# A graph layer on one core: edge loads of one chunk, eight under way, and more output rows kept to the end

## The chip, the cores and the metric

The kernel runs on one core of one Trainium2 chip. The metric is device time in microseconds of one execution. A core has five engines with instruction queues of their own: TensorE (PE in the profile; its weight loads are shown apart as PEld), VectorE (DVE), ScalarE (ACT), GpSimd (POOL) and SyncE (SP), which here only issues DMAs. SP and POOL both issue DMAs; these are carried out by the same 16 DMA engines.

## The reference

There are 12,500 nodes with 128 features and 412,500 edges with 48 features, sorted by destination node. What is computed:

```
h   = relu(layernorm(x))                            # 12500 x 128
agg = segment_sum(edge_attr, dst)                   # 12500 x 48, sums of edges by destination
u   = graph_globals[0]                              # one row of 64, for all nodes
hid = relu(concat(h, agg, u) @ W1 + b1)             # 240 -> 256
out = x + hid @ W2 + b2                             # 12500 x 128
```

All data are float32. The edges are 79.2 MB, x and the output 6.4 MB each, dst 1.65 MB.

## The kernel before, in words

**Edges.** A chunk is 896 edges: 128 partitions times T = 7 edges, 1344 B in each partition and 168 KB in all. A step `s` is 8 chunks (two halves of four), and there are NS = 58 steps; the last has a half and a tail. Because the edges are sorted, a chunk touches few nodes. DVE compares relative destinations with 0..31 (`onehot`, line 308) and so makes a 0/1 matrix. `aggregate` (334) multiplies it with the edges on TensorE, which sums the edges of each of the 32 nodes of a chunk's window. `keep_sums` (355) copies the sums with ACT, `place_columns` (372) and `place` (378) move them to their node columns with another 0/1 matrix and product, and `add` (386) adds them into `aggT`, the sums by node column, with DVE.

**Twos.** For each of the 7 edge columns `t` of a half, `aggregate` either issues four products of 32 x 48, one per chunk, or two products of 64 x 96, one per pair of chunks, of which the off-diagonal parts are not used. `LEVELS[s]` (608) says how many of the 14 columns of step `s` use the second form ("twos"): up to 7 are in the second half, the rest in the first. A step with any twos has two more small ACT copies in `keep_sums`.

**Nodes.** The rows are handled in 26 blocks: block 0 of 212 rows, 23 blocks of 512 and two of 256. Each is loaded (`load_x`, 393), normalized (DVE and ACT), turned (TensorE), multiplied with the parts of W1 (`first_h`, `first_a`) and W2 (`second`, 518), added to x + b2 by DVE (`result`, 527) and stored (`store`, 536). `plus_b2` (428) adds b2 on POOL. Blocks 0 to 4 (`FIRST`) are begun ahead of the loop, and parts of them are kept in columns of `aggT` not used yet.

**Order.** The order of all instructions is written out by hand (`tc.manual_schedule()`). A planner (`piece`, 707) puts the pieces of blocks into half-steps `k` (two to a step) and `at(k, ...)` lists them; the loop at line 854 then issues each step.

**Edge loads.** SP issues them. `load(s, i)` (297) loads one pair of chunks, 336 KB, into a tile of 2 x 1344 B per partition; there are 18 such tiles. In step `s` the loop calls `load(s + 3, i)` for i = 0..3 at four places. `few` (290) keeps at most FLIGHT = 5 loads of edges, x and dst under way: each waits for the one that is five before it to land. In the loop, each also waits for the matrix product issued last ahead of it ("in TensorE's pace").

**Stores.** For most blocks POOL issues the store half a step after `second`. The blocks in `HELD` (103), the 16 blocks 6 to 21, write their result into columns of `aggT` that are done with, and their stores come in the last three steps, three in each half-step (`k = 2 * (NS - 3) + i // 3`, line 813). Each of these also waits for the matrix product issued last ahead of it. The last three stores (blocks 23 to 25) follow the last products, one from POOL and two from SP.

Of the kernel before, what the change touches and what calls it, by code (L numbers as in the profile page):

```python
# [22 lines left out]
def kernel(  # L23
# [30 lines left out]
    CS = 2 * CH  # L54
# [7 lines left out]
    NS = NSF + 1  # L62
# [33 lines left out]
    NBL = len(blocks)  # L96
# [3 lines left out]

    FIRST = (1, 2, 3, 0, 4)

    HELD = range(NBL - 4 - 16, NBL - 4)
    ZN = 16
    zw = -(-(N + WG) // ZN)

# [36 lines left out]
    def load_edges(e, c, n):  # L143
        return nc.sync.dma_start(
            e[:, :n], edge_attr[c * CE:(c + n) * CE].rearrange("(c p t) d -> p c (t d)", p=P, t=T))
# [4 lines left out]
    def rows_of(ap, a, m, r):  # L150
        return ap[a:a + m * r].rearrange("(p r) d -> p (r d)", r=r)
# [6 lines left out]
    with fast:  # L158
# [131 lines left out]
        def few(now):  # L290
            if len(flight) == FLIGHT:
                tc.add_manual_dep(now.ins, flight.pop(0).ins.name, LANDED, reason="few loads under way")
            flight.append(now)
            if paced:
                tc.add_manual_dep(now.ins, last[0], LANDED, reason="in TensorE's pace")

        def load(s, i):
            if s >= NS or s == NSF and i > 1:
                if s == NSF and i == 2:
                    edges[s].append(etail)  # L300
                return
            for c in (2 * i,):
                e = ep.tile([P, 2, T * DE], F32, name="e")
                few(load_edges(e, s * CS + c, 2))
                edges.setdefault(s, []).extend([e[:, 0], e[:, 1]])
                both.setdefault(s, []).append(e)

# [26 lines left out]
        def aggregate(s, h, twos):  # L334
            left = s == NSF and h
            if h == 0:
                banks_s[s] = ps_agg.tile([P, 512], F32, name="ps")[:, :4 * DE].rearrange("p (h f) -> p h f", h=2)
            ps, es, oh = banks_s[s], edges[s], onehots[s]
            n = TT if left else T
            for t in range(n):  # L340
                first, end = t == 0 and h == 0, t == n - 1
                if t >= n - twos:
                    for q in range(0, CH, 2):
                        c = CH * h + q
                        product(ps[W * q:W * (q + 2), h], oh[:, c // 2, t], both[s][c // 2][:, :, t * DE:(t + 1) * DE],
                                start=first, stop=end, skip_group_check=True)
                    continue
                for q in range(1 if left else CH):
                    c = CH * h + q
                    o = DE * (q % 2) if twos else 0  # L350
                    product(
                        ps[W * q:W * (q + 1), h, o:o + DE], oh[:, c // 2, t, c % 2], es[c][:, t * DE:(t + 1) * DE],
                        start=first, stop=end, skip_group_check=True)
# [32 lines left out]
        def add(s):  # L386
            _, v = nc.values_load_multi_w_load_instructions(  # L387
                at_i[0:1, s:s + 1], engines=[DVE], min_val=low(s), max_val=high(s),
                skip_runtime_bounds_check_because="clamped to these on the chip")
            to = aggT[:HI + DE, ds(v[0], WG)]  # L390
            nc.vector.tensor_tensor(to, to, banks_p.pop(s)[:HI + DE, :WG], OP.add)  # L391
# [135 lines left out]
        def result(j):  # L527
            a, m, r = blocks[j]
            if j in HELD:
                ot = aggT[:, BEFORE + a:BEFORE + a + r * D].rearrange("p (r d) -> p r d", d=D)  # L530
# [5 lines left out]
        def store(j):  # L536
# [3 lines left out]
            for p0, p1 in by_rows(m):  # L540
                now = queue.dma_start(rows_of(out, a + p0 * r, p1 - p0, r), ov[p0:p1])  # L541
                if j in HELD:
                    tc.add_manual_dep(now.ins, last[0], LANDED, reason="edges first")
# [58 lines left out]

        AHEAD = 4
        EARLY = 2
        FLIGHT = 5


        LEVELS = (0, 0, 0, 0, 7, 0, 0, 9, 14, 3, 14, 14, 0, 14, 3, 3, 2, 0, 5, 14, 0, 14, 2, 3, 0, 4, 14, 0, 14, 2, 4, 0, 3, 0, 5, 14, 0, 14, 0, 4, 0, 2, 0, 3, 14, 0, 14, 4, 2, 2, 0, 2, 2, 4, 0, 0, 0, 0)
        LATE = NS - 7
        NEAR = len(FIRST) + 1  # L610
        with tc.manual_schedule():
# [42 lines left out]
            def load_step(s):  # L654
                for i in range(4):
                    load(s, i)
# [3 lines left out]
            load_x(FIRST[1])  # L660
            load_step(0)
            load(1, 0)
            load(1, 1)
            load_x(FIRST[2])
            load(1, 2)
# [28 lines left out]
            def at(k, f, *a):  # L694
                todo.setdefault(max(0, k), []).append((f, a))
# [48 lines left out]
            for i in range(1, len(FIRST)):  # L744
                k = 2 * i
# [38 lines left out]
            for j in range(NW):  # L784
# [8 lines left out]
                if j + 1 < NW:  # L793
                    hidden_x(j + 1)
                    at(where["o", j] + 1, result, j)
                    if j not in HELD:
                        at(where["o", j] + 1, store, j)
# [3 lines left out]
            for j in range(NBL):  # L801
                if j in FIRST:
                    continue
                k = where["turn", j]
# [5 lines left out]
                at(k - 2, normal, j)  # L810
            at(where["a", 0] - 2, bias_of_globals)
            for i, j in enumerate(HELD):
                k = 2 * (NS - 3) + i // 3
                assert where["o", j] + 1 < k
                at(k, store, j)

# [3 lines left out]
            def apart(k, f, *a):  # L820
                while k - 1 in taken or k in taken or k + 1 in taken:
                    k -= 1
                taken.add(k)
                at(k, f, *a)
                return k
# [3 lines left out]
            for i in range(2, len(parts)):  # L829
                need = 2 * (parts[i][0] // CS - (4 if i == len(parts) - 1 else 0))  # L830
                k = apart(need - 4, middles, i)
                at(k + 2, check_dst, i)
                k = apart(k - 1, spread_dst, i, 1)
                k = apart(k - 1, spread_dst, i, 0)
# [5 lines left out]
            k = apart(2 * (NS - 6), verdict)  # L840
# [13 lines left out]
            for s in range(NS):  # L854
# [27 lines left out]
                if s >= LATE:  # L882
                    for p in now:
                        place(p)
                        add(p)
                twos = [max(0, LEVELS[s] - T), min(T, LEVELS[s])]
                aggregate(s, 0, twos[0])
# [37 lines left out]
    with tc.If(isbad >= 1):  # L925
# [3 lines left out]
        with tc.tile_pool(name="any", bufs=1) as ap, tc.tile_pool(  # L929
# [63 lines left out]
            with tc.For_i(0, NCH, 1) as c:  # L993
                e = ap.tile([P, T * DE], F32, name="e2")
                nc.sync.dma_start(e, edge_attr[ds(c * CE, CE)].rearrange("(p t) d -> p (t d)", t=T))
                windows(e, rel[:, ds(c, 1), :].rearrange("p c t -> p (c t)"), ds(c, 1), P)
            e = ap.tile([P, T * DE], F32, name="e3")
# [65 lines left out]
```

## Time and profile before

| | us |
|---|---|
| median of the timed runs | 301.53 |
| timed runs | 299.49, 301.53, 303.27 |
| profiled execution, its own time | 298.43 |
| its span, first to last instruction | 296.6 |
| TensorE busy in it | 283.1 |
| VectorE, ScalarE, GpSimd busy | 237.0, 161.0, 73.7 |
| mean granted clock of TensorE | 0.991 of full speed |

A row of a table by stage holds, for a stretch of the span, the busy time of each engine with its number of instructions, then the clock that TensorE was granted, the mean busy share of the 16 DMA engines (it can pass 1, since packets of one engine overlap) and the GB/s that they moved. A row of waits says which engine and line waited for what: us in total, times, and the longest. A row of a source line gives an instruction's duration as minimum, median and maximum in ns. A row of the chain of waits gives the start, the duration in us, and what ran. A row of DMA issues gives the number of DMAs, KB of each, and the median us from issue to landing.

### The profile page before, as it was taken

How to read it: one execution, taken by the hardware profiler on the slowest of the kernel's cores; microseconds unless marked ns; L12 is line 12 of the kernel's file. 1: busy time of each engine (PE TensorE's matmuls, PEld its weight loads, DVE VectorE, ACT ScalarE, POOL GpSimd, SP SyncE). 2: the span in 40 equal slices, each digit the busy share in tenths (PEclk: the TensorE clock that was granted, in tenths of full speed). 3: DMA queues.
4: the chain of work that ended last, by engine and by line, in shares of the span. 5: the costliest groups of instructions: out<-in, count | busy, mean ns of one | idle time of the engine just before them, and what ended most of it. 6: DMA issues, size and time to landing. Idle time of an engine off the chain costs nothing.

```text
span 296.6 us, 15062 instructions
## 1 busy us (share of the span) xinstructions
PE 283.1 (95%) x6553; PEld 223.5 (75%) x6554; DVE 237.0 (80%) x537; ACT 161.0 (54%) x399; POOL 73.7 (25%) x88
## 2 busy tenths in 40 slices
PE   6799897999999999999999999999999999999992
PEld 2657666898878778878878788867877977787781
DVE  6838969699998997887978699698986799986222
ACT  3477557323756664743666458644651985664420
POOL 3032381130212563021022212021111022103720
PEclk9999998999999999999999999999999999999998
DMA  6999999999999999999999999999999999999962
GB/s 162 372 314 345 272 358 313 370 370 370 356 357 356 326 367 285 298 348 290 332 312 339 346 345 317 336 321 322 310 347 337 353 298 323 337 352 317 363 222 81
DMA packets 69815, 95.19 MB, mean 321 GB/s; under 512 B 5018, under 2 KB 64739, under 8 KB 69743
## 3 DMA queue, kind: packets, MB, share of 16 engines
q1 hardware_dynamic: 67583, 87.66, 89.1%
q0 software_dynamic: 2160, 6.50, 6.1%
q8 instruction: 53, 0.87, 1.2%
q14 instruction: 19, 0.16, 0.1%
HBM read 87.74 MB, written 6.40 MB: 317 GB/s over the span
## 4 chain that ended last, share of the span: by engine, by line
PE 81%; DVE 8%; ACT 3%; DMA 2%; issue 2%; SPq 1%; DVEq 1%
PE ps L195 30%; PE ph L195 21%; PE po L195 14%; PE pp L195 10%; PE pt L199 5%; DVE oh L312 3%; DMA e<-in_edge_attr_dram 2%; DVE place L374 2%; ACT xn L438 1%; ACT hT L452 1%; PE pt L195 1%; DVE st L408 1%; DVE aggT L391 1%; DVE ph L489 1%; DVEq L387 1%
## 5 line engine op out<-in xcount | busy, mean ns | idle before, releaser
L312 DVE TENSOR_TENSOR oh<-iota,rel 128x1792 f32<-128x1792 f32 (+1 forms) x60 | 120.5, 2009 | 0.4 <-ACT rel L270 0.4
L195 PEld LDWEIGHTS ps<-e,oh 128*32 128x32 f32 (+1 forms) x5448 | 94.7, 116 | 21.7 <-issue 5.8
L195 PE MATMUL ps<-e,oh 128*32 128x48 f32 (+1 forms) x5448 | 106.5, 217 | 3.1 <-issue 1.2
L360 ACT COPY sums<-ps 128x192 f32<-128x192 f32 (+2 forms) x129 | 36.7, 285 | 78.7 <-PE ps L195 76.8
L431 POOL TENSOR_TENSOR xb<-xt,b_sb 128x512 f32<-128x512 f32 (+1 forms) x21 | 34.2, 1630 | 131.7 <-DVE aggT L533 79.4
L195 PE MATMUL ph<-hT,w1h 128*128 128x512 f32 (+2 forms) x100 | 49.6, 602 | 0.1
L195 PE MATMUL po<-w,hid 128*128 128x128 f32 (+1 forms) x376 | 48.0, 281 | 0.9 <-ACT hid L516 0.9
L516 ACT ACTIVATE hid<-ph,bias 128x512 f32<-128x512 f32 (+2 forms) x49 | 30.4, 670 | 30.4 <-PE ph L195 22.9
L195 PEld LDWEIGHTS po<-w,hid 128*128 128x128 f32 (+1 forms) x376 | 45.1, 196 | 2.0 <-ACT hid L516 1.3
L391 DVE TENSOR_TENSOR aggT<-aggT,pp 112x246 f32 x58 | 23.6, 406 | 24.5 <-PE pp L195 18.2
L195 PE MATMUL pp<-place,sums 128*112 128x128 f32 x232 | 39.0, 291 | 0.2 <-DVE place L374 0.2
L195 PEld LDWEIGHTS pp<-place,sums 128*112 128x112 f32 x232 | 28.9, 176 | 7.1 <-issue 1.7
L438 ACT ACTIVATE xn<-xt,sh,sc 128x128 f32<-128x128 f32 x80 | 33.1, 483 | 0.3
L374 DVE TENSOR_TENSOR place<-iota,pos 128x256 f32<-128x256 f32 x58 | 32.9, 569 | 0.0
L195 PE MATMUL ph<-aggT,w1a 48*128 48x256 f32 (+1 forms) x192 | 28.6, 402 | 0.2 <-DVE aggT L391 0.2
L195 PEld LDWEIGHTS ph<-aggT,w1a 48*128 48x128 f32 x192 | 17.2, 186 | 10.1 <-issue 6.8
L452 ACT COPY hT<-pt 128x512 f32<-128x512 f32 (+1 forms) x22 | 23.0, 1044 | 3.2 <-PE pt L199 3.1
L195 PEld LDWEIGHTS ph<-hT,w1h 128*128 128x128 f32 x100 | 16.7, 196 | 7.1 <-issue 4.6
L533 DVE TENSOR_TENSOR aggT<-po,xb 128x512 f32<-128x512 f32 x16 | 11.0, 685 | 9.2 <-PE po L195 9.2
L541 POOL DMA_DIRECT2D out_dram<-ot x9 | 5.0, 553 | 51.6 <-DVE ot L533 43.7
L408 DVE BATCH_NORM_STATS2 st<-xt 128x6 f32<-128x128 f32 x80 | 17.3, 277 | 0.0
L199 PE MATMUL pt<-ident,xn 128*128 128x128 f32 x84 | 14.1, 289 | 0.0
(137 smaller groups left out, 188.1 us busy)
## 6 DMA issues: line engine op xcount, KB each, us to landing
e<-in_edge_attr_dram SPq DMA_DIRECT2D x230, 336.0 KB, 5.2
xt<-in_x_dram SPq DMA_DIRECT2D x19, 256.0 KB, 4.9
out_dram<-aggT POOLq DMA_DIRECT2D x16, 256.0 KB, 4.5
out_dram<-ot POOLq DMA_DIRECT2D x7, 256.0 KB, 4.8
di<-in_dst_dram SPq DMA_DIRECT2D x3, 448.0 KB, 5.3
aggT<-in_x_dram SPq DMA_DIRECT2D x4, 256.0 KB, 4.2
xt<-in_x_dram SPq DMA_DIRECT2D x2, 128.0 KB, 4.6
out_dram<-ot SPq DMA_DIRECT2D x2, 128.0 KB, 3.3
```

Of the source, the lines that this page charges most:

```text
L195: last[:] = [nc.tensor.matmul(*a, **k).ins.name]
L199: last[:] = [nc.tensor.transpose(*a, **k).ins.name]
L312: nc.vector.tensor_tensor(to, iota[:, None, :W].to_broadcast([P, n, W]), r[:, :, None].to_broadcast([P, n, W]), OP.is_equal)
L360: nc.scalar.copy(to[k, h], ps[k, h, None, o:o + DE].to_broadcast([k.stop - k.start, h.stop - h.start, 2, DE]))
L374: nc.vector.tensor_tensor(po, iota[:, None, :WP].to_broadcast([P, 2, WP]), pos[:, s, :, None].to_broadcast([P, 2, WP]), OP.is_equal)
L391: nc.vector.tensor_tensor(to, to, banks_p.pop(s)[:HI + DE, :WG], OP.add)
L408: nc.vector.bn_stats(st[:m, q, :], xs[j][:m, q, :])
L431: nc.gpsimd.tensor_tensor(xb[:m, :r], xs[j][:m, :r], b2_sb[:m, None, :].to_broadcast([m, r, D]), OP.add)
L438: nc.scalar.activation(xn[:m, q], xs[j][:m, q], AF.Relu, bias=shift[j][:m, q:q + 1], scale=scale[j][:m, q:q + 1])
L452: nc.scalar.copy(hT[:, :m * r].rearrange("d (p r) -> d r p", r=r), ht[j][:, :m * r].rearrange("d (r p) -> d r p", r=r))
L516: nc.scalar.activation(to, ph, AF.Relu, bias=bias[:, h:h + 1])
L533: nc.vector.tensor_tensor(ot[:m, :r], pos_o[j][:m, :r], xbs[j][:m, :r], OP.add)
```

## The change

Edge loads are issued one chunk at a time, 168 KB, into the two halves of the same tiles, and eight loads may be under way. The stores of blocks 1 to 5 join those held for the last three steps, 21 blocks, now four in each half-step. The list of twos is another one: its sum goes from 248 to 254, and the number of steps that have any from 35 to 33. The number of tiles, the planner, and the places at which loads are issued stay.

```diff
-    HELD = range(NBL - 4 - 16, NBL - 4)
+    HELD = range(1, NBL - 4)
...
             for c in (2 * i,):
                 e = ep.tile([P, 2, T * DE], F32, name="e")
-                few(load_edges(e, s * CS + c, 2))
+                for q in range(2):
+                    few(load_edges(e[:, q:q + 1], s * CS + c + q, 1))
                 edges.setdefault(s, []).extend([e[:, 0], e[:, 1]])
                 both.setdefault(s, []).append(e)
...
-        FLIGHT = 5
-
-
-        LEVELS = (0, 0, 0, 0, 7, 0, 0, 9, 14, 3, 14, 14, 0, 14, 3, 3, 2, 0, 5, 14, 0, 14, 2, 3, 0, 4, 14, 0, 14, 2, 4, 0, 3, 0, 5, 14, 0, 14, 0, 4, 0, 2, 0, 3, 14, 0, 14, 4, 2, 2, 0, 2, 2, 4, 0, 0, 0, 0)
+        FLIGHT = 8
+
+
+        LEVELS = (0, 0, 0, 0, 7, 5, 5, 14, 0, 14, 14, 3, 14, 5, 0, 4, 0, 0, 4, 0, 14, 0, 14, 4, 0, 4, 3, 14, 0, 14, 4, 0, 4, 0, 7, 14, 0, 14, 0, 4, 0, 3, 0, 14, 0, 14, 5, 3, 2, 4, 0, 0, 2, 4, 0, 0, 0, 0)
...
             for i, j in enumerate(HELD):
-                k = 2 * (NS - 3) + i // 3
+                k = 2 * (NS - 3) + i // 4
                 assert where["o", j] + 1 < k
                 at(k, store, j)
```

## The prediction

> **What bounds the kernel now.** I read the page first, then a table by stage, then the waits of TensorE, and last the queue of SP and the chain of waits. The page:
>
> ```profile
> span 296.6 us, 15062 instructions
> ...
> PE 283.1 (95%) x6553; PEld 223.5 (75%) x6554; DVE 237.0 (80%) x537; ACT 161.0 (54%) x399; POOL 73.7 (25%) x88
> ...
> DMA packets 69815, 95.19 MB, mean 321 GB/s; under 512 B 5018, under 2 KB 64739, under 8 KB 69743
> ...
> q1 hardware_dynamic: 67583, 87.66, 89.1%
> q0 software_dynamic: 2160, 6.50, 6.1%
> ...
> PE 81%; DVE 8%; ACT 3%; DMA 2%; issue 2%; SPq 1%; DVEq 1%
> ```
>
> Two resources look full: TensorE is busy 95% of the span, and the two DMA queues together keep the 16 engines busy for 95.2% of it. The table by stage tells which of them sets the pace. Its columns after the stretch are the busy us of PE, PEld, DVE, ACT and POOL, then the granted clock, the DMA share and GB/s:
>
> ```profile
> 31.60:35.00 3.40, 2.50 (x59) 1.87 (x62) 3.33 (x8) 2.28 (x5) 0.92 (x2) 1.00 0.88 230
> 45.70:49.10 3.40, 1.81 (x52) 1.44 (x40) 3.40 (x7) 1.83 (x4) 0.33 (x1) 1.00 0.96 314
> 49.10:52.50 3.40, 3.40 (x50) 3.17 (x53) 3.40 (x4) 2.47 (x8) 0.74 (x2) 0.51 0.93 291
> 49.00:105.00 56.00, 55.84 (x1257) 47.57 (x1257) 51.88 (x107) 30.33 (x79) 15.38 (x18) 0.97 1.04 354
> 105.00:160.00 55.00, 55.00 (x1258) 43.94 (x1254) 45.34 (x95) 31.31 (x76) 11.91 (x10) 1.00 0.98 320
> 160.00:215.00 55.00, 55.00 (x1401) 43.45 (x1400) 47.05 (x100) 30.27 (x74) 11.09 (x9) 1.00 1.00 328
> 215.00:270.00 55.00, 55.00 (x1377) 43.76 (x1376) 46.89 (x113) 33.80 (x91) 9.06 (x8) 1.00 1.00 335
> 274.00:288.00 14.00, 14.00 (x263) 11.17 (x250) 3.50 (x8) 4.90 (x12) 7.22 (x14) 1.00 0.87 318
> 288.00:291.00 3.00, 2.78 (x24) 2.59 (x24) 2.02 (x5) 0.47 (x1) 0.54 (x1) 1.00 0.01 3
> ```
>
> From 105 to 270 us TensorE is busy 165.00 of 165 us, and so are the DMA engines. The waits of TensorE from 12 us on hold one row that names the edges:
>
> ```profile
> PEld ps L195 <- DMA e<-in_edge_attr_dram: 0.5, 2, 0.3
> ```
>
> So in this execution every chunk of edges lands before TensorE wants it. TensorE's own stream sets the end, with the loads just ahead of it. What makes both full at once is the list of twos: a two computes two chunks in one product of 64x96 instead of two of 32x48, and that is the slower form. The chain of waits shows one step without twos (112 matrix instructions) and one with 14 (56):
>
> ```profile
> 230.61 2.46 PE ps L195 x56
> ...
> 278.54 1.33 PE ps L195 x112
> ```
>
> Fourteen twos cost 2.46 - 1.33 = 1.13 us, 0.081 us each. The list of before has 248 of them (summed from the code), about 20 us of filling that uses up TensorE's time while edges arrive.
>
> **The change part by part.**
>
> *The list of twos.* The sum rises from 248 to 254. Steps 5 and 6 get 5 each. Steps 7 to 9 go from 9, 14, 3 to 14, 0, 14, two more. From step 10 on the sum falls from 215 to 209. The last is on the path: 6 x 0.081 = -0.49 us. The two more of steps 7 to 9 cost +0.16 us. The ten of steps 5 and 6 fall where TensorE idles: from 45.7 to 49.1 us it is busy 1.81 of 3.40 us, idle for 1.59, while DVE is busy all 3.40. Ten twos are 0.81 us, so I cost them at nothing; with that cover gone they would cost +0.81. Behind this idle stretch the granted clock falls to 0.51 from 49.1 to 52.5 us, which loses 3.40 x 0.49 = 1.67 us of full-speed work on a TensorE that is busy throughout. With 0.81 us more work the idle time before it comes to 0.78 us. The stretch from 31.6 to 35.0 us, idle for 0.90 us, was followed by no fall (its own clock is 1.00 and the next fall is at 49). I take the fall as gone: -1.67 us, between -1.67 and 0 (0 if it comes all the same, a little later). The Trainium skill, "TensorE: Matmul & The Clock Gate", section "What's actually happening", says that the clock gate judges activity by free-running windows of some 3.4 us; by that the fall could turn on where the window lies, and the term would be 0 in some executions. The trace agrees with the length (0.51 over 3.4 us). Two steps fewer have twos at all, so ACT makes four small copies fewer, off the path at 54% busy.
>
> *One chunk a load, eight under way.* SP issues 460 edge loads in place of 230. Its queue, by the source view of the load's line and of the x loads' line (ns, min/median/max), and by the chain of waits:
>
> ```profile
> L144 SPq DMA_DIRECT2D e<-in_edge_attr_dram x230: 367/368/1955, 2.6 to 270.8; - x115
> L144 SPq EVENT_SEMAPHORE  x175: 17/17/28, 6.9 to 270.8; - x175
> ...
> DMA to landing us min/median/max: 4.1/5.2/6.8
> ```
>
> ```profile
> L398 SPq DMA_DIRECT2D xt<-in_x_dram x21: 340/341/1072, 43.8 to 246.0; - x21
> ```
>
> ```profile
> 3.12 0.47 SPq L144
> 3.59 0.04 issue
> ```
>
> A load of one chunk has the 128 runs of an x load, so its issue lies near 0.341 us, with a wait of 0.017 and two gaps of 0.04: 0.44 us. At worst it is the 0.47 of the first burst, with the same around it: 0.57. The time there is: 2.6 to 270.8 us, 268.2 us, less some 25 other loads at 0.44 (11 us), leaves 257 us, 0.559 us per chunk. At 0.44 SP needs 202 us and stays ahead; I take that, and no cost. What queues behind a stalled issue on SP is the next edge or x load, and behind those TensorE. The stream has to stay 0.12 us per chunk worse than my value before TensorE waits.
>
> The bytes under way fall from 5 x 336 KB to 8 x 168 KB, by 20%. With five under way a landing of 5.2 us means 5 x 344,064 B / 5.2 us = 331 GB/s, just what the stages show (320 to 335). Eight of half the size give 1.376 MB; for 328 GB/s they must land in 4.2 us. The landings:
>
> ```profile
> e<-in_edge_attr_dram SPq DMA_DIRECT2D x230, 336.0 KB, 5.2
> xt<-in_x_dram SPq DMA_DIRECT2D x19, 256.0 KB, 4.9
> out_dram<-aggT POOLq DMA_DIRECT2D x16, 256.0 KB, 4.5
> ...
> xt<-in_x_dram SPq DMA_DIRECT2D x2, 128.0 KB, 4.6
> out_dram<-ot SPq DMA_DIRECT2D x2, 128.0 KB, 3.3
> ```
>
> Most of a landing is queue: 128 KB of x behind four edge loads take 4.6 us, 128 KB of output at the quiet end 3.3. The queue ahead shrinks by the 20%, and 5.2 x 0.8 = 4.2 us. I take that value, at which the rate holds; the bounds are 3.3 us (417 GB/s, more than the engines move) and 4.7 us (between the two x loads, as if nothing in the queue shrank; 293 GB/s).
>
> Each load also ends in completions. From the two queue rows, 6.1% of 296.6 us x 16 over 2160 packets is 134 ns for 3009 B, and 89.1% over 67583 is 62.6 ns for 1297 B. The line through both is 0.042 ns a byte and 8.5 ns a packet. One small packet more per engine and load is 230 x 8.5 ns = 2.0 us of the engines' time (upper bound 230 x 62.6 ns = 14.4 us, lower 0). The packets under 512 B, 5018, fit 16 to a DMA. The rule that speaks against the change is in the Trainium skill, "DMA: Bandwidth & Descriptors", section "Rules for kernel authors": at least 1 MiB a DMA for bandwidth. Taken with that page's fit in "Anatomy of one DMA" (2.0 us fixed plus bytes over 436 GB/s), an estimate of 2.4 us a chunk with eight under way gives 575 GB/s, so overlapped loads would not be held by it; the sum stays as the rows give it.
>
> *Five more blocks' rows at the end.* Blocks 1 to 5 (256 KB each, 1.31 MB) no longer go out between 49 and 105 us. At that stage's 354 GB/s this is 3.7 us of DMA, so the edges come 3.7 - 2.0 = 1.7 us earlier there. TensorE does not wait for edges in this trace, so on the path it is worth nothing here, at most -1.7 us where it does wait. On POOL five issues leave; nothing behind them there (xb, zeroing) was late for TensorE. At the end:
>
> ```profile
> 272.16 3.21 POOL L541 DMA_DIRECT2D out_dram<-aggT  x6 [3.48 <-PE pt L199]
> ...
> 281.26 2.13 POOL L541 DMA_DIRECT2D out_dram<-aggT  x4 [1.09 <-PE ph L195]
> ```
>
> POOL issues one store in 3.21 / 6 = 0.54 us, 490 GB/s, faster than the engines drain. From 274 to 291 us the engines are idle for 0.13 x 14 + 0.99 x 3 = 4.8 us, and the 3.7 us fit in, ahead of the last three stores at 290.4. I cost this at nothing; if the stores ran over, the last output would be late by up to 3.7 us.
>
> **The sum.** -0.49 + 0.16 - 1.67 = -2.0 us on TensorE's stream. The profiled execution took 298.43 us (span 296.6), so it would take 296.4. The three timed runs of before are 299.49, 301.53 and 303.27; the mean of all four executions is 300.7, and I predict 300.7 - 2.0 = 298.7 us, 1% below the median of 301.53.
>
> **The rivals.**
>
> 1. *The fall of the clock stays, or comes elsewhere.* For it: the ten twos are only 0.81 us, 0.12 us under the one idle stretch that is known to be harmless. Against it: the idle time is halved. Then -0.3 us: 300.4.
>
> 2. *The loads gate the timed runs.* All three lie above the profiled execution, which could be TensorE waiting for edges there. Then relief on the DMA counts as well: -2.0 - 1.7 = -3.7 us, and if completions are free -5.7: 295 to 297. Against it: this trace has 0.5 us of such waits.
>
> 3. *The smaller window starves the DMA engines* (the other side). If a chunk lands in 4.7 us, the rate is 293 in place of 328 GB/s, and the 165 us from 105 to 270 become 165 x 328 / 293 = 185: +20 us, less 1.7 of relief and 2.0 of TensorE, +16: 317 us. It decides from a landing of 4.2 us on, and costs 2% (6 us) from 4.4. For it: x loads half as big land only 0.6 us sooner. Against it: 3.3 us at the quiet end.
>
> 4. *SP becomes the bound.* From 0.559 us a chunk on; at 0.57, 460 x 0.011 = +5 us less 2.0: 304. For it: issues up to 1.955 us in the row. Against it: the median of 0.368 for twice the runs.
>
> 5. *The stores run over the end*: +3.7 - 2.0: 302.
>
> **How the numbers follow.** Forecast 0.47 (296.5 to 301), rival 1 0.18, rival 2 0.15, rival 3 0.08, rival 4 0.07, rival 5 0.05. The range 294.5 to 305 takes in the forecast and rivals 1, 2, 5 and most of 4; left out are rival 3 and the edges of 2 and 4, 0.15. Two per cent of 301.53, about what a measurement of this kernel can tell from no change, is 6 us: faster means under 295.5, slower over 307.6. Faster: half of rival 2 and the low edge of the forecast and of 1, 0.16. Slower: rival 3 and the worse end of 4, 0.12. Within: 0.72.
>
> **What would show it.** Right: no clock under 1.00 between 45 and 56 us; TensorE busy all of 105 to 270; edge landings of about 4.2 us at 320 to 335 GB/s; issues near 0.34 us; packets under 512 B up by some 3,700; the last held store landed before the last three. Wrong: TensorE waits on edges in the hundreds of ns per step (rivals 3, 4: landings of 4.7 us with the DMA share below 0.95, or SP with no waits left), or a DMA share under 0.9 in the middle with TensorE full, which would mean that the filling is now too much and could be cut.

## The result, and the profile after

The changed kernel takes 326.51 us (median of four runs, 322.97 to 330.92) against 301.23 us for the kernel before on the same chip (299.49 to 303.27). The ratio is 1.0731, with a 95% interval from 1.0646 to 1.0817: 7% slower, where 298.7 us was forecast. Two runs of the changed kernel, its profiled execution of 330.92 us among them, were disturbed and are left out of the ratio; the others lie at 322.97 to 323.54 us, so the rows below tell where the time is, and the last 2% of them is not explained.

The page of the changed kernel, with the rows that answer to those of before:

```profile
span 329.2 us, 15276 instructions
...
PE 299.7 (91%) x6529; PEld 233.7 (71%) x6530; DVE 227.3 (69%) x537; ACT 159.3 (48%) x395; POOL 88.6 (27%) x88
...
DMA packets 73497, 95.22 MB, mean 289 GB/s; under 512 B 8698, under 2 KB 68419, under 8 KB 73423
...
q1 hardware_dynamic: 71263, 87.68, 84.9%
...
DMA 46%; PE 37%; SPq 8%; ACT 3%; issue 2%; DVE 2%; DVEq 0%; ACTq 0%
...
e<-in_edge_attr_dram SPq DMA_DIRECT2D x460, 168.0 KB, 4.4
out_dram<-aggT POOLq DMA_DIRECT2D x21, 256.0 KB, 6.3
```

The chain that ends last has changed hands. It was 81% TensorE and 2% DMA; now it is 46% DMA and 37% TensorE. The bytes are the same, but the mean rate has gone from 321 to 289 GB/s, and a load of half the size lands in 4.4 us where the whole one took 5.2. A stretch of the chain of waits shows what that looks like (start, duration, what ran):

```profile
109.61 4.39 DMA e<-in_edge_attr_dram
114.00 0.14 issue
114.14 1.34 PE ps L195 x26
...
118.16 0.43 SPq L144
118.59 0.04 issue
118.63 0.43 SPq L144
...
119.59 4.87 DMA e<-in_edge_attr_dram
124.47 0.04 issue
124.51 1.37 PE ps L195 x26
```

TensorE's products of a step come behind a load that took 4.39, then 4.87 us from its issue to its landing, and in the second case behind issues on SP, one after the other. TensorE itself stands for a part of that time. In its waits from 12 us on, the row that named the edges with 0.5 us before is now this:

```profile
PEld ps L195 <- DMA e<-in_edge_attr_dram: 20.6, 34, 2.4
```

Over the whole span, by the source view of the load's line:

```profile
  PEld ps L195: 21.8, 38
...
  PE ps L195: 16.2, 27
...
DMA to landing us min/median/max: 2.9/4.4/8.9
```

The weight loads of TensorE wait 21.8 us for edges and its products 16.2; these waits overlap in time and can't be added. SP's own waits for landings have nearly gone; the row of before comes first, then that of the changed kernel:

```profile
SPq L144 <- DMA e<-in_edge_attr_dram: 108.2, 176, 2.4
```

```profile
SPq L144 <- DMA e<-in_edge_attr_dram: 11.0, 23, 1.1
```

So SP has little time to spare, and the eight places are not always full. The table by stage says how the loss is spread (busy us of PE, PEld, DVE, ACT and POOL, then granted clock, DMA share, GB/s):

```profile
33.90:37.30 3.40, 3.40 (x61) 3.04 (x50) 2.27 (x3) 0.38 (x2) 1.10 (x1) 0.51 1.05 349
49.10:52.50 3.40, 3.40 (x67) 3.28 (x65) 3.40 (x4) 2.63 (x8) 1.04 (x2) 1.00 1.01 323
49.00:105.00 56.00, 52.42 (x1250) 43.50 (x1249) 46.23 (x95) 26.05 (x65) 16.09 (x12) 1.00 0.99 315
105.00:160.00 55.00, 52.84 (x1125) 41.30 (x1127) 41.18 (x93) 28.34 (x71) 15.37 (x9) 1.00 0.97 301
215.00:270.00 55.00, 52.05 (x1250) 40.42 (x1251) 42.01 (x104) 29.41 (x80) 11.58 (x7) 1.00 0.96 303
300.00:329.20 29.20, 17.72 (x182) 14.02 (x182) 3.57 (x8) 3.17 (x8) 6.49 (x12) 0.68 0.48 185
```

From 49 to 105 us the rate is 315 GB/s, where it was 354, and from there to 270 us some 300, where it was 328. In before, 56 x 354 + 165 x 328 GB/s make 73.9 MB from 49 to 270 us. The changed kernel has moved 56 x 315 = 17.6 MB of that by 105 us and needs 56.3 MB / 300 GB/s = 187.6 us for the rest: it is there at 292.6 us, 22.6 us later. Two things are left out, and they cancel: it came to 49 us with 1.3 MB less (280 GB/s against 306), and 1.3 MB of stores are put off to the end. The difference of its other runs to before is of the same size (323.5 - 301.2 = 22.3), but the rates are those of the profiled execution, which is 32.6 us longer than that of before, so that the close match is in part luck.

TensorE still shows as 91% busy. Its busy time has risen from 283.1 to 299.7 us with 24 matrix instructions fewer. Part of that is the lower clock of this execution (0.966 against 0.991), and the rest looks like waiting that is counted as busy. The number of matrix instructions is the better reading of progress: 3,544 from 105 to 270 us, where before had 4,032.

### The profile page after: what moved, and what is told of

The parts are those of the page before. It is cut to its first block, busy times and chain, and to the rows that moved or that the text cites. A ratio compares the mean times of both kernels' runs of the same rounds, so it can differ in the third digit from the quotient of the medians.

```text
span 329.2 us, 15276 instructions
## 1 busy us (share of the span) xinstructions
PE 299.7 (91%) x6529; PEld 233.7 (71%) x6530; DVE 227.3 (69%) x537; ACT 159.3 (48%) x395; POOL 88.6 (27%) x88
## 2 busy tenths in 40 slices
DMA packets 73497, 95.22 MB, mean 289 GB/s; under 512 B 8698, under 2 KB 68419, under 8 KB 73423
## 4 chain that ended last, share of the span: by engine, by line
DMA 46%; PE 37%; SPq 8%; ACT 3%; issue 2%; DVE 2%; DVEq 0%; ACTq 0%
DMA e<-in_edge_attr_dram 43%; PE ps L195 15%; PE ph L195 9%; SPq L144 8%; PE po L195 6%; PE pp L195 5%; PE pt L199 2%; DMA xt<-in_x_dram 2%; DMA aggT<-in_x_dram 1%; ACT xn L439 1%; ACT hT L453 1%; DVE st L409 1%; PE pt L195 1%; DVE aggT L392 0%; SPq L399 0%
## 5 line engine op out<-in xcount | busy, mean ns | idle before, releaser
L195 PE MATMUL ps<-e,oh 128*32 128x48 f32 (+1 forms) x5424 | 120.6, 219 | 17.6 <-DMA e<-in_edge_attr_dram 16.2
L195 PEld LDWEIGHTS ps<-e,oh 128*32 128x32 f32 (+1 forms) x5424 | 102.8, 117 | 42.1 <-DMA e<-in_edge_attr_dram 21.8
L313 DVE TENSOR_TENSOR oh<-iota,rel 128x1792 f32<-128x1792 f32 (+1 forms) x60 | 117.3, 1956 | 0.4 <-ACT rel L270 0.4
L432 POOL TENSOR_TENSOR xb<-xt,b_sb 128x512 f32<-128x512 f32 (+1 forms) x21 | 49.2, 2341 | 176.0 <-DMA xt<-in_x_dram 126.2
L361 ACT COPY sums<-ps 128x192 f32<-128x192 f32 (+2 forms) x125 | 35.8, 287 | 111.7 <-PE ps L195 110.2
L195 PE MATMUL ph<-hT,w1h 128*128 128x512 f32 (+2 forms) x100 | 50.6, 613 | 0.1
L195 PE MATMUL po<-w,hid 128*128 128x128 f32 (+1 forms) x376 | 47.5, 280 | 0.8 <-ACT hid L517 0.8
L195 PE MATMUL pp<-place,sums 128*112 128x128 f32 x232 | 40.0, 296 | 0.2 <-DVE place L375 0.2
L195 PEld LDWEIGHTS pp<-place,sums 128*112 128x112 f32 x232 | 29.8, 181 | 7.3 <-issue 2.0
L375 DVE TENSOR_TENSOR place<-iota,pos 128x256 f32<-128x256 f32 x58 | 25.4, 440 | 0.0
L542 POOL DMA_DIRECT2D out_dram<-aggT x21 | 11.3, 544 | 9.9 <-DMA out_dram<-aggT 5.8
```

Source lines behind the costliest of these rows:

```text
L195: last[:] = [nc.tensor.matmul(*a, **k).ins.name]
L313: nc.vector.tensor_tensor(to, iota[:, None, :W].to_broadcast([P, n, W]), r[:, :, None].to_broadcast([P, n, W]), OP.is_equal)
L361: nc.scalar.copy(to[k, h], ps[k, h, None, o:o + DE].to_broadcast([k.stop - k.start, h.stop - h.start, 2, DE]))
L375: nc.vector.tensor_tensor(po, iota[:, None, :WP].to_broadcast([P, 2, WP]), pos[:, s, :, None].to_broadcast([P, 2, WP]), OP.is_equal)
L432: nc.gpsimd.tensor_tensor(xb[:m, :r], xs[j][:m, :r], b2_sb[:m, None, :].to_broadcast([m, r, D]), OP.add)
```

## The experiments

Theory A: the bytes under way (1.376 MB instead of 1.72) hold the rate down, since a landing does not shrink in proportion. Theory B: SP's time for twice the issues does. Theory C: the small packets and completions of twice the loads do. Theory D: the list of twos or the held stores do. Edits are made to the kernel before. From most runs the row of the stretch from 105 to 270 us is shown; that of before is

```profile
105.00:270.00 165.00, 165.00 (x4032) 131.15 (x4028) 139.27 (x308) 95.39 (x239) 32.05 (x26) 1.00 0.99 328
```

**The loads alone, and all but the loads.** The first run has only the loads of the change:

```diff
-                few(load_edges(e, s * CS + c, 2))
+                for q in range(2):
+                    few(load_edges(e[:, q:q + 1], s * CS + c + q, 1))
...
-        FLIGHT = 5
+        FLIGHT = 8
```

> The kernel before with only the loads changed (one chunk each, eight under way); the old list of twos and the old 16 held blocks. All three theories of the slow loads (SP's issue; the engines' own cost per load; fewer bytes under way) expect most of the loss here: 316 to 324 us, with edge landings near 4.4 us and about 300 GB/s in the middle. If the stores or the list made the loss, 300 to 303.

Measured: 325.98 us against 301.03, ratio 1.084 (1.0715 to 1.0966).

```profile
105.00:270.00 165.00, 157.38 (x3544) 123.98 (x3543) 123.38 (x282) 87.66 (x219) 39.95 (x28) 0.98 0.95 299
```

That is the whole loss, a little more than the 316 to 324 us expected. The other has the new list of twos (its lines are cut here) and the 21 held blocks, with the loads of before:

```diff
-    HELD = range(NBL - 4 - 16, NBL - 4)
+    HELD = range(1, NBL - 4)
...
-        LEVELS = (0, 0, 0, 0, 7, 0, 0, 9, 14, 3, 14, 14,
+        LEVELS = (0, 0, 0, 0, 7, 5, 5, 14, 0, 14, 14, 3,
...
-                k = 2 * (NS - 3) + i // 3
+                k = 2 * (NS - 3) + i // 4
```

> The changed kernel with the loads put back to pairs of chunks, five under way; the new list and the 21 held blocks stay. By the terms of the prediction for these two (fall of the clock gone -1.67, list -0.33, stores hidden) 298 to 300 us, about 2 below before. If the stores collide with the last edges by themselves, 303 or more.

Measured: 301.67 us against 301.03, ratio 1.0063 (1.0012 to 1.0114).

```profile
34.60:38.00 3.40, 3.40 (x57) 2.94 (x45) 2.15 (x3) 0.47 (x2) 0.00 (x0) 0.50 1.06 349
```

The whole loss is in the loads: theory D falls. The list and the held rows do not bring the 2 us expected either, and the fall of the clock is still there, earlier in the execution (0.50 from 34.6 to 38.0 us, where before has 1.00).

**The same bytes under way with the DMAs of before.** Pairs as before, but four of them:

```diff
-        FLIGHT = 5
+        FLIGHT = 4
```

> The kernel before with four pairs under way in place of five: 1.376 MB, the same bytes under way as eight single chunks, with half as many DMAs. The window theory expects the loss here too: about 300 GB/s, 315 us or more. The issue theory and the engine theory expect no change: landings fall to some 4.2 us, the rate stays 320 to 335 GB/s, 300 to 304 us.

Measured: 329.88 us against 301.03, ratio 1.1024 (1.0914 to 1.1134). The stretch, and then from the page:

```profile
105.00:270.00 165.00, 156.35 (x3549) 123.66 (x3550) 123.24 (x278) 88.45 (x222) 46.33 (x28) 0.98 0.95 300
```

```profile
q1 hardware_dynamic: 67583, 87.66, 84.5%
...
e<-in_edge_attr_dram SPq DMA_DIRECT2D x230, 336.0 KB, 4.6
```

This is the run that decides. It has the issues of before on SP (230) and the packets of before (67,583), so neither B nor C has anything to work with: the smaller window alone is enough for the loss. It may have as many bytes under way as the changed kernel, 4 x 344,064 = 1.376 MB, and it has its rate (300 GB/s), its count of matrix instructions (3,549), and its loss. Four pairs in 4.6 us are 299 GB/s.

**The window put back.** Every other pair is loaded as two singles, with six and with eight loads under way. A load has 229 KB on average, so these are 1.376 and 1.835 MB:

```diff
-                few(load_edges(e, s * CS + c, 2))
+                if i % 2:
+                    for q in range(2):
+                        few(load_edges(e[:, q:q + 1], s * CS + c + q, 1))
+                else:
+                    few(load_edges(e, s * CS + c, 2))
...
-        FLIGHT = 5
+        FLIGHT = 6
```

> The kernel before, in which of the four pair loads of a step two stay pairs and two are split into single chunks; six loads under way, 1.376 MB on the mean, with 345 edge loads. SP has 1.5 issues per pair, well under its limit. The window theory expects the same loss as with four pairs or eight singles: landings such that about 300 GB/s flow, 320 to 330 us. The issue theory expects 300 to 304, the engine theory (a cost per load) about half of the loss, 312.

Measured with six: 318.4 us against 300.88, ratio 1.0576 (1.0507 to 1.0644).

```profile
105.00:270.00 165.00, 155.82 (x3651) 122.99 (x3639) 123.96 (x283) 89.04 (x224) 49.74 (x29) 1.00 0.95 301
```

The same with FLIGHT = 8:

> The same mixed loads with eight under way, 1.83 MB on the mean, somewhat more than the 1.72 MB of before. The window theory expects the rate of before or a little more and 300 to 304 us, although half of the chunks are loaded singly. The engine theory expects half of the loss, about 312, whatever the window.

Measured: 303.91 us against 300.88, ratio 1.0187 (1.0079 to 1.0294).

```profile
105.00:270.00 165.00, 161.85 (x3819) 126.79 (x3818) 133.29 (x301) 91.70 (x231) 29.93 (x25) 1.00 0.98 319
```

These two differ in the window alone and have the same 345 issues. The window is worth 14.5 us between them, and 301 against 319 GB/s. The 1.9% that remains to before may be issues and completions (115 loads more than before, where the changed kernel has 230 more), or what a window wider than 1.72 MB costs by itself, of which more below.

**SP's time.** Is SP harmless, then? Eight empty instructions were put on SP behind each load of a pair:

```diff
                 few(load_edges(e, s * CS + c, 2))
+                for _ in range(8):
+                    nc.sync.drain()
```

> The kernel before with eight empty instructions (drains, some 0.055 us each by the end of the trace of before) on SP behind each pair load: SP's time for a pair goes from about 0.48 to 0.92 us, near that of two single loads (2 x 0.48), with no DMA added. The issue theory expects the loss of the single loads: 312 us or more, SP hardly waiting for landings. The engine and window theories expect 300 to 303 us, with SP's waits for landings cut by about 100 us in total.

Measured: 310.31 us against 301.03, ratio 1.0337 (1.0236 to 1.0437).

```profile
105.00:270.00 165.00, 161.82 (x3818) 128.32 (x3817) 134.45 (x303) 91.84 (x233) 35.55 (x27) 0.99 0.98 317
```

So time on SP does cost, though only a third of the loss and less than the 312 us that theory B asked for. SP waited 12.6 us for landings here, against 108.2 in before: it comes late to a free place, and the window is not full. The other way round, SP was relieved. In the kernel of the first run, every second chunk was issued from ACT's queue:

```diff
-        return nc.sync.dma_start(
+        return (nc.scalar if n == 1 and c % 2 else nc.sync).dma_start(
```

> Single chunks, eight under way, as in the run with the loads alone, but every second one is issued by ACT, so that SP issues 230 edge loads as before the change. The issue theory expects SP's relief to bring back most of the 25 us: 300 to 306. The window theory expects little, since the bytes under way are still at most 1.376 MB: at best the mean under way rises from 7.2 to 8 loads, 315 to 326 us; ACT, which was busy for 161 us, may lose some on top.

Measured: 356.11 us against 302.04, ratio 1.1835 (1.1652 to 1.2018). From the waits:

```profile
PEld ps L195 <- DVE oh L313: 17.3, 2, 15.8
```

The edit did something else as well. TensorE stands for 15.8 us at the start behind a DVE result, with ACT's queue now holding loads that wait for landings in front of ACT's own work (argued from the order on the queue). The run says nothing on SP's share. It was repeated with every fourth chunk from POOL, which has more room:

```diff
-        return nc.sync.dma_start(
+        return (nc.gpsimd if n == 1 and c % 4 == 3 else nc.sync).dma_start(
```

> Single chunks, eight under way, as in the run with the loads alone, but every fourth one is issued by POOL: SP has 345 edge loads. POOL, busy for 74 us, has room for 115 issues of some 0.54 us, though a store or an xb ahead of one in its queue may hold it up. The issue theory expects most of the loss back: 300 to 306. The window theory expects 316 to 326: at most 1.376 MB under way.

Measured: 329.76 us (322.67 to 331.55) against 300.56; its runs lie too far apart for a ratio. The stretch and SP's wait for landings:

```profile
105.00:270.00 165.00, 154.85 (x3552) 121.86 (x3550) 124.00 (x274) 85.28 (x215) 66.73 (x88) 0.99 0.94 299
```

```profile
SPq L144 <- DMA e<-in_edge_attr_dram: 84.0, 105, 4.4
```

SP now has 84.0 us in which it waits for landings (13.1 in the first run), and the rate is 299 GB/s as it was. The places were no fuller for it: by the times of issue and landing in the traces, 7.3 loads were under way on the mean from 105 to 270 us, and 7.2 in the first run. With ten under way (1.72 MB, as in before) in place of eight:

> The same with ten under way, 1.72 MB, the bytes of five pairs. The window theory expects the loss to go: 300 to 306. The engine theory (a cost per load) expects no change against eight: 316 or more. If POOL's queue holds its share up, both of these runs are slow, and then they tell nothing.

Measured: 315.31 us against 300.56, ratio 1.0506 (1.0425 to 1.0588).

```profile
30.00:49.00 19.00, 17.35 (x403) 12.73 (x392) 12.54 (x18) 9.76 (x24) 11.40 (x17) 0.95 0.83 253
...
105.00:270.00 165.00, 159.71 (x3798) 126.12 (x3795) 131.95 (x300) 92.89 (x231) 74.13 (x98) 1.00 0.98 324
```

With the window of before the rate of before is nearly back in this stretch, 324 GB/s, though all loads are single chunks. The time is not: 300 to 306 us were expected. The 5% that stays is spread: the rate is 253 GB/s from 30 to 49 us (318 in before), and TensorE is idle for 5.3 us in the long stretch (0 in before). How much of it is POOL's issues and how much completions was not taken apart. More than eight from SP alone was not tried.

The runs with loads of one size can be put side by side by the bytes that were under way on the mean from 105 to 270 us, and the mean landing of an edge load. Both are worked out from the times of issue and landing in the traces; for up to half of the loads the traces do not tell the landing, and the median of the run is put in.

| | MB under way | landing, us | GB/s |
|---|---|---|---|
| every fourth of eight singles from POOL | 1.30 | 4.4 | 299 |
| changed kernel | 1.33 | 4.4 | 300 |
| four pairs | 1.37 | 4.6 | 300 |
| five pairs, empty instructions on SP | 1.51 | 4.7 | 317 |
| every fourth of ten singles from POOL | 1.52 | 4.7 | 324 |
| five pairs (before) | 1.69 | 5.2 | 328 |

The rate goes with the bytes under way, whether the loads are pairs or singles. SP's time belongs to the same account: a late SP leaves places empty (7.4 of eight are used in the changed kernel, 4.5 of five with the empty instructions). How much of the changed kernel's loss would go with a faster SP was not separated.

**More under way than five pairs.** If the window holds the rate down, does before want a wider one? FLIGHT = 8, FLIGHT = 6, and FLIGHT = 6 with the new list and the held rows:

```diff
-        FLIGHT = 5
+        FLIGHT = 8
```

> The kernel before with eight pairs under way in place of five. From the two landings 4.6 us at 1.37 MB (four pairs) and 5.2 us at 1.70 MB (five), the window theory makes 2.2 us plus 1.77 us per MB, so 7.0 us at 2.75 MB and 390 GB/s, above what the engines have moved in any stage (about 370): the engines become the limit of the loads. TensorE's own stream with its twos is then alone in setting the end: 297 to 300 us. If the engines were already full at five, landings rise to 8.3 us and nothing changes: 300 to 302.

> The kernel before with six pairs under way, 2.06 MB. By the window theory the loads get faster (350 GB/s where they are not paced), but TensorE's stream already hides them at five: 299 to 302. With eight pairs TensorE waited more for what the profile calls issue (12.8 us in place of 7.0); if those are its instructions, fetched behind the edges, six lie between: 300 to 304.

> The changed kernel with pairs and six under way (21 held blocks, the new list). With the middle of the run relieved of five stores and a larger window, no wait for edges should be left: 298 to 301 if the rest of the change is worth anything at all, 301 to 304 if it is not.

Measured: eight 304.11 us against 302.04, ratio 1.0173 (1.0047 to 1.0299); six 301.67 against 300.88, ratio 1.0059 (1.0013 to 1.0104); six with list and held rows 302.61 against 300.88, ratio 1.0021 (0.9972 to 1.0071). With eight, by stage:

```profile
49.00:105.00 56.00, 54.34 (x1249) 46.04 (x1248) 51.59 (x107) 30.19 (x79) 15.37 (x18) 1.00 1.04 361
105.00:270.00 165.00, 162.43 (x3906) 128.41 (x3906) 135.32 (x302) 93.00 (x232) 29.65 (x25) 1.00 0.98 317
```

The loads are a little faster where they are free to run (361 against 354 GB/s), and then TensorE sets the pace. The wider window is not filled there: 5.1 loads were under way on the mean from 105 to 270 us, about as many as in before, since each load also waits for TensorE's products. Nothing is gained beyond five, and four lose 10%. With eight the time rather rises (297 to 302 us were expected), and TensorE's waits for "issue" with it (at the end). None of the runs beats before.

**The twos.** Are they filling, as the prediction has it? All out (the line of before is cut here), with five and with eight pairs under way:

```diff
-        LEVELS = (0, 0, 0, 0, 7, 0, 0, 9, 14, 3, 14, 14,
+        LEVELS = (0,) * NS
```

> The kernel before with no twos at all: 20 us less work for TensorE (248 x 0.081), loads as before. With five pairs the window holds the loads at about 330 GB/s, so the window theory expects TensorE to wait for edges about as long as it filled: 297 to 302 us, perhaps with falls of the clock. If the loads had slack and TensorE's stream alone set the time, 281 to 285.

> No twos and eight pairs under way. The window theory expects the rate to rise to 350 to 370 GB/s and TensorE to use its 20 us: 281 to 288 us, faster than both kernels. If the engines were full at five pairs, 297 to 302 like the run without twos and with five.

Measured: 325.2 us against 302.04, ratio 1.0802 (1.0622 to 1.0981), and with eight 325.13, ratio 1.0759 (1.055 to 1.0967). By the window theory I had expected 297 to 302 and 281 to 288: both are misses, and the gain of the second is not there. Views of the first, the page and the waits, and then the row of before on queue 8:

```profile
PE 274.5 (85%) x7545; PEld 214.0 (66%) x7546; DVE 236.1 (73%) x537; ACT 140.8 (43%) x329; POOL 72.6 (22%) x88
...
q8 instruction: 60, 0.98, 1.2%
```

```profile
PEld ps L195 <- issue: 38.0, 40, 3.7
...
PE ps L195 <- issue: 29.6, 26, 3.6
...
PEld ps L195 <- DMA e<-in_edge_attr_dram: 1.3, 2, 0.7
```

```profile
q8 instruction: 53, 0.87, 1.2%
```

TensorE has 8.6 us less busy time and a thousand more instructions (7,545 against 6,553), and its weight loads stand for 38.0 us and its products for 29.6 (overlapping in time), up to 3.7 us at a time, on nothing that these rows name. In before the same two rows have 5.8 and 1.2 us. So the twos do not fill time: with them the stream of instructions is shorter, and these waits are not there.

What the waits are for can be read from the packets. Queue 8, which the profile calls "instruction", carries packets of 16 KB, seven more of them than in before. In the two runs without twos there are 51 stretches over 0.7 us, from 12 us on, in which weight loads and products both stand, 76 us together; 47 of them end 1.2 to 1.65 us after a packet of queue 8 has ended. Only 9% of moments taken at random lie like that. So TensorE waits there for its own instructions.

## Why the prediction was wrong, point by point

**The step that failed** is the landing of a single load: "The queue ahead shrinks by the 20%, and 5.2 x 0.8 = 4.2 us. I take that value, at which the rate holds". It took a landing for queue alone, so that a smaller window costs nothing whatever its size. The row beside it spoke against that: 3.3 us for 128 KB at the quiet end is a landing without a queue. The runs show that a large part does not shrink. Before and the four pairs give two points, 1.72 MB in 5.2 us and 1.376 MB in 4.6 us. The line through them is 0.6 / 0.344 = 1.74 us per MB and a rest of 5.2 - 1.72 x 1.74 = 2.2 us. (Both landings are rounded to 0.1 us, so the rest lies between 1.7 and 2.7.) Two points always make a line; the table in the experiments tests it. With 1.33 MB under way on the mean it gives 4.5 us for the changed kernel, and 4.4 were measured; with 1.51 MB it gives 4.8 for the empty instructions, measured 4.7; with 1.52 MB it gives 4.8 for the ten singles, measured 4.7. The changed kernel is below four pairs in bytes, since SP did not always keep all eight places filled: 8 x 172,032 B / 4.4 us are 313 GB/s, and 300 were moved. The Trainium skill, "DMA: Bandwidth & Descriptors", section "Anatomy of one DMA", has a fixed 2.0 us for each DMA, mostly the completion. It says so of DMAs that GpSimd issues; these are SP's, and the rest of 2.2 us agrees in size. From that page's fit for one DMA alone I had concluded that overlapped loads would not be held by the fixed part; they are, since the places under way are few.

**The bounds held the value, 4.4 us; the choice between them was wrong.** The profile's row of 128 KB of x behind edge loads in 4.6 us was the nearest row to a small load in the busy stretch, and gave the upper bound of 4.7. The stores at the quiet end (3.3 us) stand in no queue and should not have pulled the value down. For 4.4 us the text had a price of 2%; 7% came, since the eight places were not always full and the stage before lost rate too.

**Rival 3** (the smaller window starves the engines; 317 us, chance 0.08) is what happened. It was priced for the stretch from 105 to 270 us alone. The stage before it also lost rate, 354 to 315 GB/s, which is 56 x 354 / 315 - 56 = 7 us more; with that it would have said 324. That this is so near is luck: its landing of 4.7 us was too long, and the 3.7 us that it took off did not come. With the rates measured, 300 and 315 GB/s, the two stages give 15.4 + 6.9 = 22.3 us. What made the loss full was in the first view: the loads were "just ahead" of TensorE, so that 8.5% of rate (300 for 328) has no cover.

**Rival 4** (SP becomes the bound) is not needed for the loss: four pairs, with half the issues and SP waiting 140.7 us for landings, lose at least as much. But SP has a part. The median issue was 0.424 us and not 0.341, so that a chunk takes SP some 0.52 us with the wait and the gaps of the prediction, near its limit of 0.559. And the prediction's bound, that SP costs nothing until it is full, is wrong: the empty instructions on SP cost 3% with half the issues, since a place in the window that is free stays empty until SP comes to it. The signs that the prediction named for rivals 3 and 4 (TensorE waiting on edges, SP with hardly a wait left) came together and could not tell them apart.

**The completions**, +2.0 us of the engines' time, could not be separated. The count was right (8,698 - 5,018 = 3,680 small packets more, 3,700 forecast), and the four pairs lose as much without them.

**The list, the clock and the held rows**, -2.0 us together, gave +0.6% (0.1 to 1.1) in the run without the loads. The largest term, the fall of the clock, failed as rival 1 has it: the fall at 49 us went, and one came at 34 us (0.51 in the changed kernel, 0.50 without its loads). With eight pairs neither stretch has one. With nothing changed but the number of pairs under way, the fall is at 49 us with five, at 46 with six, and not there with eight; with four the first is at 147. The Trainium skill, "TensorE: Matmul & The Clock Gate", section "What's actually happening", has free-running windows; these runs do not speak against it, though none repeats one kernel, and a single fall is not to be entered in a sum. The six twos (0.49 us) are below what the runs can tell. The prediction's word "filling" for the twos was wrong (the last pair of runs).

**The stores at the end** cost nothing that can be seen where the loads are in time (+0.6% in all for the run without the loads). In the changed kernel they meet the last edges and land in 6.3 us; the loads alone, with 16 held blocks, lose as much, so this is not the cause.

**Rival 2** (relief on the DMA counts) falls with the run without the small loads: it has the 3.7 us of stores taken out of the middle, and is not faster.

## What to carry to other kernels

When loads overlap, count the bytes under way and not the loads: the rate is the bytes under way over the landing, and a landing has a part (2.2 us of 5.2 here) that does not shrink with the window. When loads are made smaller, their number has to rise until the bytes are the same again, and the engine that issues them must keep the places full: here ten singles with POOL's help still lost 5%. Before doing any of it, price one fewer of the old loads in a single run. A busy share of DMA near 1 with landings much longer than a lone one does not prove a queue that can be cut.

## What the runs showed of the hardware

The busy share of the DMA engines is no measure of their capacity. Four pairs move the same 87.66 MB in the same 67,583 packets as five, and the packets took 84.5% of 328.0 us = 277 us where they took 89.1% of 296.6 = 264: fewer bytes under way made the same packets longer by 5%, at a share of 0.95 and 8.5% less rate.

TensorE can lose time that the profile calls "issue" to the fetching of its own instructions. Without twos, 7,545 matrix instructions in place of 6,553, its weight loads stood so for 38.0 us and not 5.8, and 47 of 51 long stretches ended 1.2 to 1.65 us after a 16 KB packet of the queue "instruction". The bytes of that queue fit TensorE's stream: 0.98 MB for 15,091 products and weight loads, 0.87 MB for 13,107, some 65 B each. A likely reason, an estimate from these numbers: a packet holds some 250 instructions, and a step without twos goes through 112 products and as many weight loads in 1.33 us, while a packet takes 1.07 us on the mean and TensorE goes on 1.2 us and more after its end. A step of 14 twos has half the instructions in 2.46 us. Whether edge loads delay the packets stays open: the packets themselves took no longer than in before (1.11 us), but with eight pairs under way the waits of the weight loads are longer (47.5 us in place of 38.0 without twos, 8.8 in place of 5.8 with them).
